# Routing pieces at the end of the first attention: exponentials traced one step later, divisions two steps later, some pieces in other steps

## The chip, the cores and the metric

The kernel runs on one core of a Trainium2 chip. The metric is the device time of one execution in microseconds. The core has five engines with a queue each: TensorE (PE, whose weight loads appear as PEld), VectorE (DVE), ScalarE (ACT), GpSimd (POOL) and SyncE (SP, which issues the DMAs). An instruction starts when it is at the head of its engine's queue and its semaphore waits are met, so an instruction that waits holds all that stand behind it on that engine.

## The reference

Two layers act on x, of shape (8, 256, 256) in float32, each an attention and a feed-forward part added to x. The change lies where the first attention (layer 0, 16 heads of 16) ends and the first mixture of experts begins to be routed. What matters of the reference:

```python
def _L0_ffn_ref(x, norm_gamma, slot_norm_gamma, slot_embeds, w1, b1, w2, b2):
    xn = rmsnorm(x, norm_gamma)
    sn = rmsnorm(slot_embeds, slot_norm_gamma)
    logits = jnp.einsum('bnd,esd->bnes', xn, sn)
    dispatch = jax.nn.softmax(logits, axis=1)
    b, n, e, s = logits.shape
    combine = jax.nn.softmax(logits.reshape(b, n, e * s), axis=-1)
    slots = jnp.einsum('bnd,bnes->besd', xn, dispatch)
    h = jnp.einsum('besd,edh->besh', slots, w1) + b1[None, :, None, :]
    h = jax.nn.gelu(h, approximate=False)
    eo = jnp.einsum('besh,ehd->besd', h, w2) + b2[None, :, None, :]
    out = jnp.einsum('bmd,bnm->bnd', eo.reshape(b, e * s, -1), combine)
    return out

x = x + _L0_xattn_ref(_layernorm(x, axis=-1), ctx_768, ...)
x = x + _L0_ffn_ref(_layernorm(x, axis=-1), ...)
x = x + _L1_xattn_ref(_layernorm(x, axis=-1), ctx_768, ...)
x = x + _L1_ffn_ref(_layernorm(x, axis=-1), ...)
```

There are 8 experts with 128 slots each, so the logits of a batch are 256 tokens x 1024 slots. The routing of one batch is two softmaxes over them: one along the slots for each token (combine), one along the tokens for each slot (dispatch), and from the second the contents of the slots.

## The kernel before

All of x stays in SBUF (x_sb). The program runs layer 0's attention for 8 batches, then the mixture of experts in 4 groups of 2 batches, then layer 1's attention and its feed-forward part.

**The loop of the first attention.** The outer loop `for h in range(8 * B + 12)` (from L868) makes 76 steps. A step h traces: `scores` (L525), which holds TensorE's scores of step h by query (for the row maxima, NM on DVE) and by key (for step h-6, whose exponentials ex on ACT are L573); `turn_back`; the second halves of pieces begun in the step before (`for f in halves`); every fourth step `pair_maxima` (nm on TensorE, added to QT on DVE); the pieces that `whole` lists for step h, entered with `at(h, f)`; and every fourth step `values` (o on TensorE, zt and rz on DVE, zs on POOL). From step 64 on there are only scores by key, from step 70 on none.

**What sets the order.** Instructions made through `matmul`, `transpose` and, inside the loop, `vec` (DVE) and `gps` (POOL) are kept in program order on their engine, and so are the score exponentials. Other ACT instructions (the copies and, before, the routing's exponentials) and operations made after the loop, such as the scaling xh_moe of later batches (through `normed`, L233), are placed by a scheduler, which can bring them forward among the loop's. All through `vec` and `gps` are recorded under L103, so tiles tell them apart. Readers of one PSUM tile on different engines take turns: each waits for the one before it.

**PSUM.** Scores use two buffers ("big"). All else that TensorE writes in the loop, but o, shares three 128x512 buffers (`ps_mm`); a group waits until the buffer that it takes has been read.

**The routing of batches 0 and 1 (`routing0`, L729)** is spread over steps 43 to 75 as pieces. A plan is a string: a letter for the piece, the step, and arguments after the point. For each batch:

- N (`scale`): xh_moe, the normalized tokens, two operations on POOL.
- P (`prepare`): four transposes pt_xm, two scaled copies xnT on DVE.
- T (`by_token` t, m): logits ln of token half t and slot half m; maximum nmn on DVE; copy of the logits on ACT into se (L760); with m = 1 the minimum of both negated maxima, two exponentials of 512 columns with their sums (L766), the sum zn and its inverse rzn on DVE.
- U (`turn_token` t): eight transposes ptn, two copies to CT, one on ACT (L784) and one on DVE.
- S (`by_slot` q, h): four transposes ls of the copied logits of both token halves, maxima nms on DVE, two exponentials of 256 columns (L807), the inverse of their sums (zs) on DVE, and the division by it on POOL.
- D (`turn_slot` q): eight transposes pts, two copies on ACT (L830) into the tile wq.
- F (`fill` q, c): two matmuls pf, then four scaled writes into the slots, alternately on ACT (L848) and DVE.

The exponentials go in turn into three parts of tiles that the attention no longer needs: two halves of krows and wk. `slot_scaled` and `slot_piece` make the scaled transposed slot embeddings snT, `moe_mean` the means and variances of later groups' tokens (bst, mvp), and `moe_scale_newton` their scales: three instructions on DVE and then sixteen small ones on POOL (nt, ny, scl). The weights of the first expert are loaded in step 50. After the loop the experts begin (ph, L1060; ht on ACT, L1068, which needs another activation table).

**Where the steps lie in the profiled execution.** Step 47's scores start at 161.12 us, step 50's at 173.54, step 54's at 189.44, step 55's at 194.22, step 60's at 212.84, step 63's at 226.92, step 66's at 235.43, step 69's at 247.74, and the first ph at 271.71.

Of the kernel before, what the change touches and what calls it, by code (L numbers as in the profile page):

```python
# [8 lines left out]
F32 = mybir.dt.float32  # L9
# [6 lines left out]
P = 128  # L16
# [47 lines left out]
def kernel(ctx: ExitStack, tc: tile.TileContext, a: dict, out: bass.AP):  # L64
# [219 lines left out]
    with ExitStack() as l0:  # L284
# [444 lines left out]
        def routing0(b):  # L729
# [14 lines left out]
            def by_token(t, m):  # L744
# [16 lines left out]
                if m == 1:  # L761
                    vec.tensor_tensor(nm[:, 2:3], nm[:, 0:1], nm[:, 1:2], ALU.min)
                    en = st[f"en{t}"] = next_em()
                    z = stat.tile([P, 4], F32, tag="zm", bufs=4, name=f"zn_{b}_{t}")
                    for i in range(2):
                        nc.scalar.activation(  # L766
                            en[:, i * 512 : (i + 1) * 512],
                            lgs[t][i],
                            AF.Exp,
                            bias=nm[:, 2:3],  # L770
                            accum_out=z[:, i : i + 1],
                        )
                    vec.tensor_tensor(z[:, 2:3], z[:, 0:1], z[:, 1:2], ALU.add)
                    vec.reciprocal(rzn0[:, 2 * b + t : 2 * b + t + 1], z[:, 2:3])
# [14 lines left out]
            def by_slot(q, h):  # L789

                if h == 0:
                    st[f"es{q}"] = next_em().rearrange("p (i n) -> p i n", i=4)
                    st["nms"] = stat.tile([P, 4], F32, tag="nm", bufs=4, name=f"nms_{b}_{q}")
                    st["zs"] = stat.tile([P, 4], F32, tag="zm", bufs=4, name=f"zs_{b}_{q}")
                es, nm, z = st[f"es{q}"], st["nms"], st["zs"]
# [9 lines left out]
                for i in range(2):  # L805
                    k = 2 * h + i
                    nc.scalar.activation(  # L807
                        es[:, k, :],
                        pl[:, i, :],
                        AF.Exp,  # L810
                        bias=nm[:, k : k + 1],
                        accum_out=z[:, k : k + 1],
                    )
                vec.reciprocal(z[:, ks], z[:, ks])
                gps.tensor_tensor(
                    es[:, ks, :],
                    es[:, ks, :],
# [844 lines left out]
```

## Time and profile before

| | us |
|---|---|
| median of 3 runs (lowest, highest) | 1348.21 (1345.59, 1351.38) |
| time of the profiled execution | 1348.56 |
| its span, first to last instruction | 1346.8 |
| busy PE / PEld | 1316.7 / 955.1 |
| busy DVE / ACT / POOL | 562.4 / 582.1 / 245.1 |
| mean granted clock | 0.997 |

A line of the profile names the engine, the kernel's line, the operation, the tiles written and read, and the sizes. What stands in brackets at the end of a row of the timeline is the idle time of that engine before the row, and whose work ended it. A row of the waits gives the waiting engine, tile and line, what it waited for, the total in us, how often, and the longest. A row of the windows gives start and end in us, the length, the busy time and instruction count of each engine, the mean granted TensorE clock (1.00 is full), the DMAs' busy share, and GB/s. Rows of PE count passes, of which one matmul in float32 has two or more, so "x4" can be two instructions.

### The profile page before, as it was taken

The page shows a single profiled execution, that of the slowest core. Times are in us where ns is not written, and L with a number is a line of the kernel's source. Part 1 is how long each engine was busy: PE and PEld are TensorE (multiplying, and loading weights), DVE is VectorE, ACT ScalarE, POOL GpSimd, SP SyncE. Part 2 cuts the span into 40 slices and gives each one's busy share as a digit, 9 for nine tenths or more (in the row PEclk, how much of TensorE's full clock was granted, in tenths as well). Part 3 has the DMA queues.
Part 4 walks back from the last instruction along what each step waited for, and adds up shares of the span by engine and source line. Part 5 has one row for each costly group of instructions (what it writes and reads, how often), then busy time and mean ns, then how long its engine had stood idle before and what let it go on. Part 6 is the DMA issues. An engine that isn't in the chain of part 4 may idle for free.

```text
span 1346.8 us, 19104 instructions
## 1 busy us (share of the span) xinstructions
PE 1316.7 (98%) x7520; PEld 955.1 (71%) x7520; DVE 562.4 (42%) x1118; ACT 582.1 (43%) x1406; POOL 245.1 (18%) x285
## 2 busy tenths in 40 slices
PE   8999989799999999999999999999999999999998
PEld 5666655477778877878768788876666676677777
DVE  6677766423330233321333110024545444544675
ACT  2644455544432263522625222213546445444653
POOL 3232401301010000100001000011333323333423
PEclk9999998999999999999999999999999999999999
DMA  7100000033325232432323425350000000000001
GB/s 220 60 1 2 1 1 1 1 106 125 107 93 178 88 105 96 133 129 71 129 71 133 133 67 187 113 153 1 1 1 1 1 0 1 1 1 1 1 8 55
DMA packets 59129, 86.85 MB, mean 64 GB/s; under 512 B 3360, under 2 KB 49056, under 8 KB 59040
## 3 DMA queue, kind: packets, MB, share of 16 engines
q1 hardware_dynamic: 58464, 85.11, 19.4%
q8 instruction: 59, 0.97, 0.3%
q10 hardware_dynamic: 576, 0.52, 0.1%
q14 instruction: 30, 0.25, 0.1%
HBM read 83.53 MB, written 2.10 MB: 64 GB/s over the span
## 4 chain that ended last, share of the span: by engine, by line
PE 91%; ACT 4%; DVE 3%; POOL 1%; issue 1%; DMA 1%; ACTq 0%; DVEq 0%; POOLq 0%
PE ph L1060 17%; PE pe L1076 16%; PE sc L74 9%; PE q L74 6%; PE o L74 6%; PE po L74 5%; PE k L74 5%; PE pe L77 4%; PE v L74 4%; PE pc L1102 4%; PE ln L924 3%; PE pf L1006 3%; PE pk L74 1%; PE pr L74 1%; PE pf L74 1%; PE pv L74 1%
## 5 line engine op out<-in xcount | busy, mean ns | idle before, releaser
L1068 ACT ACTIVATE ht<-ph,b 128x256 f32<-128x256 f32 x256 | 119.3, 474 | 372.1 <-PE ph L1060 371.7
L1060 PE MATMUL ph<-slots,w 128*128 128x256 f32 x1024 | 266.6, 384 | 1.9 <-ACT ht L1068 1.4
L1076 PE MATMUL pe<-w,ht 128*128 128x256 f32 x1024 | 263.1, 381 | 0.0
L1060 PEld LDWEIGHTS ph<-slots,w 128*128 128x128 f32 x1024 | 182.3, 189 | 55.0 <-ACT ht L1068 22.3
L1076 PEld LDWEIGHTS pe<-w,ht 128*128 128x128 f32 x1024 | 192.1, 190 | 29.9 <-DVE slots L1085 4.2
L1335 POOL TENSOR_TENSOR ex<-ex,rz 128x1024 f32<-128x1024 f32 x64 | 119.8, 1893 | 230.0 <-DVE rz L1333 222.5
L1322 ACT ACTIVATE ex<-sc,nm 128x256 f32<-128x256 f32 x256 | 117.4, 484 | 53.0 <-DVE nm L1317 53.0
L74 PE MATMUL sc<-KT,QT 17*128 17x256 f32 (+1 forms) x1024 | 103.3, 382 | 0.9 <-ACT QT L517 0.9
L984 POOL TENSOR_TENSOR es<-es,zs 128x1024 f32<-128x1024 f32 x12 | 22.7, 1893 | 444.8 <-DVE zs L983 444.8
L573 ACT ACTIVATE ex<-sc 128x512 f32<-128x512 f32 x128 | 75.2, 597 | 63.7 <-PE sc L74 56.8
L103 DVE TENSOR_REDUCE NM<-sc 128x2 f32<-128x512 f32 x128 | 86.5, 688 | 34.3 <-PE sc L74 30.3
L1085 DVE TENSOR_TENSOR slots<-pe,b 128x512 f32<-128x512 f32 x32 | 22.1, 692 | 185.1 <-PE pe L1076 185.1
L74 PE MATMUL q<-xT,wq 128*128 128x256 f32 x384 | 94.9, 391 | 0.9 <-DVE xT L1232 0.9
L74 PEld LDWEIGHTS sc<-KT,QT 17*128 17x128 f32 (+1 forms) x1024 | 75.8, 187 | 20.7 <-issue 11.6
L74 PEld LDWEIGHTS q<-xT,wq 128*128 128x128 f32 x384 | 69.2, 189 | 28.1 <-issue 15.2
L1317 DVE TENSOR_REDUCE nm<-sc 128x4 f32<-128x1024 f32 x64 | 75.4, 1219 | 7.7 <-PE sc L74 4.7
L74 PE MATMUL po<-wo,ot 128*128 128x256 f32 x320 | 72.5, 382 | 0.0
L77 PE MATMUL pe<-ident,ex 128*128 128x128 f32 x512 | 70.1, 278 | 0.8 <-DVE et L1351 0.7
L74 PEld LDWEIGHTS po<-wo,ot 128*128 128x128 f32 x320 | 60.1, 190 | 10.9 <-issue 3.2
L77 PEld LDWEIGHTS pe<-ident,ex 128*128 128x128 f32 x512 | 56.4, 140 | 15.3 <-issue 7.6
L1351 ACT COPY et<-pe 128x512 f32<-128x512 f32 x64 | 37.5, 598 | 63.9 <-PE pe L77 63.4
L74 PE MATMUL o<-et,V 128*64 128x256 f32 x512 | 62.8, 385 | 0.8 <-ACT ot L1370 0.8
(224 smaller groups left out, 1668.9 us busy)
## 6 DMA issues: line engine op xcount, KB each, us to landing
w<-in_w_dram SPq DMA_DIRECT2D x64, 1024.0 KB, 5.6
b<-in_b_dram SPq DMA_DIRECT2D x32, 128.0 KB, 6.8
x_sb<-in_x_dram SPq DMA_DIRECT2D x3, 512.0 KB, 6.0
ctx0T<-in_ctxT_dram SPq DMA_DIRECT2D x4, 256.0 KB, 8.2
ctx1T<-in_ctxT_dram SPq DMA_DIRECT2D x8, 128.0 KB, 7.9
se<-in_slots_dram SPq DMA_DIRECT2D x1, 1024.0 KB, 10.2
wq<-in_wq_dram SPq DMA_DIRECT2D x1, 1024.0 KB, 5.0
wo<-in_wo_dram SPq DMA_DIRECT2D x1, 1024.0 KB, 12.5
```

Of the source, the lines that this page charges most:

```text
L74: tc.keep_in_program_order(nc.tensor.matmul(out, lhsT=lhsT, rhs=rhs, start=start, stop=stop))
L77: tc.keep_in_program_order(nc.tensor.transpose(out, in_, ident))
L103: ins = op(*args, **kwargs)
L573: nc.scalar.activation(ex[:, 2 - 2 * i : 4 - 2 * i, :], sc[1 - i][:, :, 1, :], AF.Exp)
L924: nc.tensor.matmul(pl[:, m * 512 : (m + 1) * 512], lhsT=st["xnT"][:, c, t * P : (t + 1) * P], rhs=snT[:, c, m * 512 : (m + 1) * 512], star ...
L1060: nc.tensor.matmul(ph, lhsT=c_["w1"][:, c, hc * P : (hc + 1) * P], rhs=slots[e][:, c * 256 : (c + 1) * 256], start=(c == 0), stop=(c == 1),)
L1068: nc.scalar.activation(ht, ph, AF.Gelu, bias=b1[:, e, hc : hc + 1])
L1076: nc.tensor.matmul(c_["pe"][:, b, :], lhsT=c_["ht"][hc][:, b * SL : (b + 1) * SL], rhs=c_["w2"][:, hc, :], start=(hc == 0), stop=(hc == HI ...
L1102: nc.tensor.matmul(pc[:, :D], lhsT=CT[:, bl, e, t * P : (t + 1) * P], rhs=eos[e][:, bl, :], start=(e == 0), stop=(e == E - 1),)
L1317: nc.vector.tensor_reduce(nm, sc, AX.X, ALU.max, negate=True)
L1322: nc.scalar.activation(ex[:, i, qb, :], sc[:, i, qb, :], AF.Exp, bias=nm[:, i, qb : qb + 1], accum_out=z[:, i, qb : qb + 1],)
L1335: nc.gpsimd.tensor_tensor(ex, ex, rz.rearrange("p h q -> p (h q)").unsqueeze(2).to_broadcast([P, 4, S]), ALU.mult,)
```

## The change

`by_token` and `by_slot` no longer issue their exponentials where they are traced. They return a function that the loop runs in the next step, behind that step's scores and score exponentials; it issues the routing's exponentials, now kept in program order on ACT, and returns a second function (the sum and inverse, or the inverse and the division), which the loop runs one step later still. The exponentials' PSUM tile of `by_slot` is read one step later, accordingly. In `fill`, the four writes of a call go to one engine: DVE for batch 1 and for batch 0 where c equals q, else ACT. In `turn_slot`, the second copy of batch 1 goes to DVE. The steps of pieces change: the slot pieces of experts 6 and 7 (sn and pt_sn) come from steps 47 and 49 to 43 and 45, `moe_scale_newton(1)` from 68 to 63 and `moe_scale_newton(2)` from 71 to 75, two pieces of `moe_mean` by two steps, and the plans as the diff shows.

```diff
         for e2 in range(4):
-            at(23 + 8 * e2, lambda e2=e2: slot_scaled(e2))
-            at(25 + 8 * e2, lambda e2=e2: slot_piece(e2))
-        for g, when in enumerate(((29, 31, 37, 39), (45, 47, 53, 61), (61, 64, 65, 66))):
+            at((23, 31, 39, 43)[e2], lambda e2=e2: slot_scaled(e2))
+            at((25, 33, 41, 45)[e2], lambda e2=e2: slot_piece(e2))
+        for g, when in enumerate(((29, 31, 37, 39), (47, 49, 53, 61), (61, 64, 65, 66))):
...
-        at(68, lambda: moe_scale_newton(1))
-        at(71, lambda: moe_scale_newton(2))
+        at(63, lambda: moe_scale_newton(1))
+        at(75, lambda: moe_scale_newton(2))
...
                 vec.tensor_reduce(nm[:, m : m + 1], pl, AX.X, ALU.max, negate=True)
                 nc.scalar.copy(lgs[t][m], pl)
-                if m == 1:
-                    vec.tensor_tensor(nm[:, 2:3], nm[:, 0:1], nm[:, 1:2], ALU.min)
+                if m == 0:
+                    return None
+                vec.tensor_tensor(nm[:, 2:3], nm[:, 0:1], nm[:, 1:2], ALU.min)
+
+
+                def exponentials():
                     en = st[f"en{t}"] = next_em()
                     z = stat.tile([P, 4], F32, tag="zm", bufs=4, name=f"zn_{b}_{t}")
                     for i in range(2):
-                        nc.scalar.activation(
...
-                    vec.tensor_tensor(z[:, 2:3], z[:, 0:1], z[:, 1:2], ALU.add)
-                    vec.reciprocal(rzn0[:, 2 * b + t : 2 * b + t + 1], z[:, 2:3])
+                        tc.keep_in_program_order(
+                            nc.scalar.activation(
...
+                    def inverse():
+                        vec.tensor_tensor(z[:, 2:3], z[:, 0:1], z[:, 1:2], ALU.add)
+                        vec.reciprocal(rzn0[:, 2 * b + t : 2 * b + t + 1], z[:, 2:3])
+
+                    return inverse
+
+                return exponentials
...
             def by_slot(q, h):
...
                 vec.tensor_reduce(nm[:, ks], pl, AX.X, ALU.max, negate=True)
...
+                def exponentials():
+                    if h == 0:
+                        st[f"es{q}"] = next_em().rearrange("p (i n) -> p i n", i=4)
+                        st["zs"] = stat.tile([P, 4], F32, tag="zm", bufs=4, name=f"zs_{b}_{q}")
+                    es, z = st[f"es{q}"], st["zs"]
...
+                    def divide():
+                        vec.reciprocal(z[:, ks], z[:, ks])
+                        gps.tensor_tensor(
...
+                    return divide
+
+                return exponentials
...
-                    nc.scalar.copy(dt[:, t, :], pt)
+                    (vec.tensor_copy if b and t else nc.scalar.copy)(dt[:, t, :], pt)
...
-                    if i % 2:
+                    if b or c == q:
                         vec.tensor_scalar(slots, got, gam[:, c : c + 1], None, ALU.mult)
...
-                "N43 P47 T48.00 T49.10 S50.00 S51.01 T52.01 T53.11 U54.0 D55.0 U55.1 F56.00 F57.01 "
-                "S58.10 S59.11 D60.1 F61.10 F63.11",
-                "N59 P62 T64.00 T65.10 S66.00 S67.01 T67.01 T68.11 D69.0 U69.0 S70.10 S71.11 U71.1 "
-                "F72.00 F73.01 D74.1 F74.10 F75.11",
+                "N43 P47 T48.00 T49.10 S50.00 S51.01 T52.01 T53.11 D54.0 U55.0 U55.1 F56.00 F57.01 "
+                "S58.10 S59.11 D62.1 F63.10 F65.11",
+                "N55 P60 T61.00 T64.10 S65.00 S66.01 T67.01 T68.11 D69.0 U69.0 U70.1 S70.10 S70.11 "
+                "F71.00 F72.01 D73.1 F73.10 F74.11",
...
-            for f in halves:
-                f()
+            later = [g for g in [f() for f in halves] if g]
...
-            halves = [g for g in [f() for f in whole.get(h, ())] if g]
+            halves = later + [g for g in [f() for f in whole.get(h, ())] if g]
```

More of the change, by code (lines that the diff above doesn't have):

```diff
@@ L765, in by_token @@
                     for i in range(2):
[L766 to L771, printed above, removed]
-                        )
-                    vec.tensor_tensor(z[:, 2:3], z[:, 0:1], z[:, 1:2], ALU.add)
-                    vec.reciprocal(rzn0[:, 2 * b + t : 2 * b + t + 1], z[:, 2:3])
+                        tc.keep_in_program_order(
+                            nc.scalar.activation(
+                                en[:, i * 512 : (i + 1) * 512],
+                                lgs[t][i],
+                                AF.Exp,
+                                bias=nm[:, 2:3],
+                                accum_out=z[:, i : i + 1],
+                            )
+                        )
+                    def inverse():
[3 more added lines that the diff above has]
+                return exponentials
             def turn_token(t):
@@ L791, in by_slot @@
                 if h == 0:
-                    st[f"es{q}"] = next_em().rearrange("p (i n) -> p i n", i=4)
                     st["nms"] = stat.tile([P, 4], F32, tag="nm", bufs=4, name=f"nms_{b}_{q}")
-                    st["zs"] = stat.tile([P, 4], F32, tag="zm", bufs=4, name=f"zs_{b}_{q}")
-                es, nm, z = st[f"es{q}"], st["nms"], st["zs"]
+                nm = st["nms"]
                 pl = ps_mm(f"ls_{b}_{q}_{h}").rearrange("p (i n) -> p i n", i=2)
@@ L804, in by_slot @@
                 vec.tensor_reduce(nm[:, ks], pl, AX.X, ALU.max, negate=True)
[L805 to L817, printed above, removed]
-                    z[:, ks].unsqueeze(2).to_broadcast([P, 2, S]),
-                    ALU.mult,
-                )
+                def exponentials():
[3 more added lines that the diff above has]
+                    es, z = st[f"es{q}"], st["zs"]
+                    for i in range(2):
+                        k = 2 * h + i
+                        tc.keep_in_program_order(
+                            nc.scalar.activation(
+                                es[:, k, :],
+                                pl[:, i, :],
+                                AF.Exp,
+                                bias=nm[:, k : k + 1],
+                                accum_out=z[:, k : k + 1],
+                            )
+                        )
+                    def divide():
+                        vec.reciprocal(z[:, ks], z[:, ks])
+                        gps.tensor_tensor(
+                            es[:, ks, :],
+                            es[:, ks, :],
+                            z[:, ks].unsqueeze(2).to_broadcast([P, 2, S]),
+                            ALU.mult,
+                        )
+                    return divide
+                return exponentials
             def turn_slot(q):
```

## The prediction

> **What bounds the kernel now.** I read the page first. TensorE is the bound over the whole span:
>
> ```profile
> span 1346.8 us, 19104 instructions
> PE 1316.7 (98%) x7520; PEld 955.1 (71%) x7520; DVE 562.4 (42%) x1118; ACT 582.1 (43%) x1406; POOL 245.1 (18%) x285
> ```
>
> The profiled execution took 1348.56 us, that is 1.76 around its span and 0.35 above the median of the runs (1348.21). All sums below are made against 1348.56. Adding or removing TensorE work is not part of this change, so only TensorE's idle time and its clock can move. The busy time by stretch shows where these are: TensorE is nearly full until about 165 us and again from 275.
>
> ```profile
> 155.00:165.00 10.00, 10.00 (x104) 6.49 (x100) 8.01 (x16) 5.13 (x8) 5.53 (x8) 1.00 0.01 2
> 185.00:195.00 10.00, 7.50 (x92) 4.29 (x84) 6.03 (x17) 6.64 (x15) 0.00 (x0) 1.00 0.01 2
> 215.00:225.00 10.00, 8.62 (x46) 4.48 (x46) 5.01 (x13) 4.40 (x9) 3.45 (x3) 0.66 0.01 2
> 255.00:265.00 10.00, 5.96 (x30) 2.91 (x22) 4.82 (x15) 3.51 (x12) 5.65 (x19) 1.00 0.00 0
> ```
>
> (The columns are PE, PEld, DVE, ACT, POOL, then the granted clock.) That is steps 47 to 75, which the change edits. The waits of TensorE between 155 and 275 us:
>
> ```profile
> PE sc L74 <- ACT ex L573: 3.6, 3, 1.7
> PE ptn L77 <- ACT wq L830: 2.4, 2, 1.9
> PE pf L74 <- ACT wk L807: 2.2, 1, 2.2
> PE pts L77 <- POOL wk L103: 1.6, 1, 1.6
> PE pts L77 <- POOL krows L103: 1.6, 1, 1.6
> PE ph L1060 <- ACT ht L1068: 1.1, 1, 1.1
> PE ln L74 <- DVE snT L103: 1.1, 1, 1.1
> ```
>
> With three below 0.6 they make 14.9 us. Three rows of the timelines show the rest of what I need: a queue head that waits (DVE), and the clock after a wait (PE).
>
> ```profile
> 187.80 0.16 DVE L103 TENSOR_TENSOR zn<-zn 128x1 f32<-128x1 f32 x1 [1.87 <-ACT wk L766]
> 252.74 1.38 DVE L103 TENSOR_SCALAR xh_moe<-x_sb,mvp_moe,scl 128x256 f32<-128x256 f32 x4 [3.81 <-POOL scl L103]
> 219.62 3.78 PE L74 MATMUL pf<-wq,xh_moe 128*128 128x512 f32 x4
> ```
>
> The same four pf passes take 1.88 at 199.51. Between 217 and 223 us the clock is 0.50, after 1.59 us of wait. That stretch costs 1.9 (pf), 1.0 (the sixteen score passes, 2.08 for 1.08) and 0.5 (six pts), 3.4 in all. At 247.74 eight score passes take 1.19 for 0.71, so 0.5 more. Lost now: 14.9 + 3.4 + 0.5 = 18.8.
>
> **What each part takes away.** The slot transposes pt_sn go from step 49 to 45 (0.5 us of TensorE in either place). The wait for snT, 1.06, goes. POOL scales them ahead of its Newton steps: 1.83 more there, hidden, since xh_moe was ready at 158.4 and read at 164.0.
>
> In steps 52 to 55 DVE's queue stood behind the sum zn. The chain of waits goes ex routing (1.53 on ACT), zn, the two maxima NM (1.19), one score exponential, TensorE: waits of 1.75 and 0.75. As the changed kernel is built, zn comes two steps later and the score exponentials come first. I walked each queue with the rows' durations (score exponential 0.50, routing pair 1.03 or 1.53, NM 0.60, copies 0.60, division 1.04, slots 0.27 when four follow each other). On the clock of that walk, which starts at step 47, TensorE is ready for step 54's scores at 186.2 and the last exponential of the step before at 185.7. For step 55 it is 190.2 against 188.9. So 2.5 goes; what is late next is the copy of ptn behind the score exponentials in step 55: 0.4 (0.5 now).
>
> The divisions of slots 4 to 7 end one step earlier relative to their transposes: step 60's wait of 1.59 goes, and the 3.4 of slow clock with it. The cover is thin: on the walk the second division ends near 214.9 and pts start at 215.0, so each 0.1 of lateness costs 0.1. Beside it, in step 61, two short groups (nm, pt_xm) stand ahead of the scores; where that happens now (90.94, 116.19) the scores wait 0.39 for ex. I take 0.4.
>
> Evictions: eight slots writes and two copies go from ACT to DVE, some 8 x 0.35 + 2 x 0.6 = 4.0 us on DVE and 4.1 off ACT, in stretches where DVE is busy 3 to 6 of 10. One effect is on the path: the last slots write on ACT now stands behind the table load, and ph waits 1.10 for its buffer. With these on DVE that goes. The remaining waits, 236.90 to 266.44 (8.1, and the 0.5 at 247.74), give way to the next list. One of them is the 1.63 of pts in step 74: the division of wk stood on POOL behind the sixteen operations of moe_scale_newton(2) (259.76 to 264.24). That goes to step 75, behind the last division; its reader, xh_moe_4, then holds DVE's queue until about 265, and xnT_2, the next that TensorE needs, is due near 271, so it is hidden; without that cover it costs up to the chain's 4.6. The product xh_moe of batch 1 goes to step 55 (2.43 on POOL, read in step 60, some 16 us later, hidden), the maxima pieces moe_mean (0.55 each on DVE) stay inside DVE's idle time. No DMA changes place: the expert's load stays in step 50, and SP's queue is the same.
>
> **What it adds.** First, moe_scale_newton(1) goes from step 68 to 63. As built, the first write of xh_moe_2 stands on DVE right behind the Newton start, ahead of QT0_7, nmn and the copies that follow. From ny's end to xh_moe the row above and its POOL chain (248.14 to 252.74) give 4.6 us. There ny ends 221.4, xh_moe_2 starts 226.0, QT0_7 227.0, the maximum nmn of ln_1_1_0 ends 228.5, ACT's copy se 229.1. TensorE has been ready for ls (which reads that copy) since 226.2. So 3.0 us of wait, and 0.25 at the next scores, whose exponentials queue behind the copy. If the cover were complete this were nothing; if POOL were late with zs it would be longer by as much. Today the same block stands at 248.9 to 252.7 and is partly covered.
>
> Second, steps 69 and 70 take four ptn groups in a row. ACT has, between them and the last ln, copy, exponentials, routing pair, copy, exponentials, routing pair, copy: 0.5 + 1.0 + 1.5 + 0.5 + 1.0 + 1.5 + 0.55 = 6.6 us, against 5.35 of TensorE from ln_1_0_1's end (0.75 of start-up on ACT's side): waits of 0.2 and 2.05. Third, in step 73 the divisions follow zt, ot and four slots writes on DVE (recips at 252.0), 1.04 each on POOL: pts waits 0.95 and 0.8, pf 0.15. Sum of the new waits: 0.4 + 0.4 + 3.25 + 2.25 + 1.9 = 8.2.
>
> 18.8 - 8.2 = 10.6. Each stall that goes also saves a refill of about 0.1 (13 now, 9 then): 11.0. Added up step by step, the walk gives 12.2; that is the upper end. The lower end, if every margin below 0.5 were missed by 0.5 (five places), is 8.5. At an unchanged clock: 1348.6 - 11.0 = 1337.6.
>
> **The clock.** The row at 216.38 shows that a wait of 1.59, amid transposes and score passes, halved the clock for 6.8 us; 1.75 behind ln (189.44) and 2.24 behind pf (261.44) did not. The new 3.0 wait, followed by ls, scores, ls until o starts at 231.1, is nearer to the first: I take one such stretch, 3.4. So 1341.0. [...]
>
> **The rivals.** (a) No slow stretch, 1337.6: for it speak the four longer waits without one (1.63 to 2.24); against it, that the new wait is longer than all of them.
>
> (b) Two slow stretches: steps 69 and 70 hold nothing but transposes and waits from 240.4 to 246.7. A second one costs 2.8 (3.4 less what the waits of step 73 take up): 1343.8. Against it: 248.9 to 253.3 in the trace is of the same kind, 1.89 wait included, and kept its clock; for it: the new one is 2 us longer. [...]
>
> (c) Slower than before: the clock, halved in step 65, does not recover while steps 66 to 75 stay sparse. TensorE works 26 us there; doubled, less 4.4 of waits that vanish in it, 22 us: 1359. It passes the kernel before from 22 us at half clock on (0.5 us per us). Against it: the stretch at 217 ended after 6.8 us with scores and pf alone.
>
> (d) The change does not do what it says: the score exponentials are late for another reason than the routing's place on ACT, and the waits of 1.75, 0.75 and 0.5 stay: 1341.0 + 3.0 = 1344.0. Against it is the zn row.
>
> **How the numbers follow.** Main case 0.45, (a) 0.12, (b) 0.34, (c) 0.05, (d) 0.04. About 0.5% (6.7 us) is what a measurement of this kernel can tell from no change, so faster means below 1341.5. The main case, 1341.0 with some 1.5 either way, is below it 6 times in 10: 0.28; with (a) 0.12 and 0.03 of (b), faster 0.43. Slower is (c), 0.05. Same is the rest, 0.52. The range runs from (a) less 1.2, the walk's upper end, to (b) with the 2.5 of missed margins: 1336.4 to 1346.3.
>
> **What would show it.** Right: no PE wait on snT; none on ex in steps 53 to 55; no pts wait near 215; a PE wait of about 3 on se (L760) near 226 to 229, behind a DVE wait of 4 to 4.6 on scl; clock 0.5 for about 7 us after it; a ptn wait near 2 on ACT's wq copy near 243; pts waits on POOL wk below 1; no wait of ph on ht; first ph near 264 instead of 271.7. Wrong: waits on ex left in steps 53 to 55, a covered Newton chain, or a clock row unlike the one forecast.

## The result, and the profile after

The changed kernel takes 1339.17 us (median of 6 runs, 1338.05 to 1339.90), the kernel before beside it 1348.60 (6 runs, 1345.50 to 1351.38). The ratio is 0.9933, with a 95% interval of 0.9919 to 0.9947: faster by 0.5 to 0.8%. Forecast was 1341.0. The profiled execution took 1339.66, 8.90 less than the profiled one of before. One execution of the experiments below, the profiled one of the first, ran at a mean granted clock of 0.834, 7 or 8 tenths in every slice of its page (1522.73 us), and is in no ratio.

The first lines of the page, and the waits of TensorE between 155 and 275 us (waiting engine, tile and line, what it waited for; total us, times, longest):

```profile
span 1337.9 us, 19105 instructions
...
PE 1315.6 (98%) x7520; PEld 954.9 (71%) x7520; DVE 565.3 (42%) x1128; ACT 576.8 (43%) x1396; POOL 245.7 (18%) x285
```

```profile
PE ls L77 <- ACT se L760: 1.6, 1, 1.6
PE pts L77 <- POOL wk L103: 1.6, 2, 1.0
PE ptn L77 <- ACT wq L855: 1.5, 1, 1.5
PE ls L77 <- DVE QT L103: 0.6, 1, 0.6
PE ptn L77 <- ACT CT L796: 0.4, 1, 0.4
PE sc L74 <- ACT ex L573: 0.4, 1, 0.4
PE pf L74 <- ACT wq L855: 0.3, 1, 0.3
PE ph L1084 <- ACT ht L1092: 0.2, 1, 0.2
```

They make 6.6 us where 14.9 stood. The waits on snT and on krows are gone, those on ex shrank from 3.6 to 0.4. The busy time by stretch shows the same (start and end, then PE, PEld, DVE, ACT, POOL, granted clock, DMA share, GB/s):

```profile
185.00:195.00 10.00, 9.57 (x111) 6.34 (x110) 7.98 (x20) 8.20 (x19) 4.10 (x4) 1.00 0.01 2
215.00:225.00 10.00, 10.00 (x86) 5.18 (x87) 4.55 (x12) 5.86 (x13) 3.26 (x14) 1.00 0.00 0
225.00:235.00 10.00, 7.78 (x48) 3.64 (x50) 6.18 (x18) 3.57 (x9) 0.64 (x3) 0.75 0.01 2
...
255.00:265.00 10.00, 8.16 (x32) 5.28 (x32) 5.25 (x18) 0.86 (x2) 2.93 (x7) 1.00 0.05 5
```

Between 185 and 195, TensorE went from 7.50 to 9.57 of 10. The slow clock of 215 to 225 (0.66 before) is gone, and a new one stands at 225 to 235 (0.75). The timelines of DVE and of TensorE show where that came from:

```profile
221.11 0.17 DVE L103 TENSOR_SCALAR ny_moe<-nt_moe 128x8 int32<-128x8 int32 x1
225.90 0.41 DVE L103 TENSOR_SCALAR xh_moe<-x_sb,mvp_moe,scl 128x256 f32<-128x256 f32 x1 [4.62 <-POOL scl L103]
226.22 0.68 DVE L103 TENSOR_TENSOR QT<-nm,QT 128x512 f32<-128x512 f32 x1
```

```profile
226.96 0.33 PE L77 MATMUL ls<-ident,se 128*128 128x128 f32 x1 [0.61 <-DVE QT L103]
228.89 0.55 PE L77 MATMUL ls<-ident,se 128*128 128x128 f32 x3 [1.60 <-ACT se L760]
229.39 1.71 PE L74 MATMUL sc<-QT,KT 18*128 18x256 f32 x8
231.04 1.12 PE L77 MATMUL ls<-ident,se 128*128 128x128 f32 x4
232.08 3.64 PE L74 MATMUL o<-ex,V 128*32 128x256 f32 x32
```

DVE's queue head, the first write of xh_moe_2, waits 4.62 us for POOL. QT, nmn and through it ACT's copy se are late behind it, TensorE waits 0.61 and 1.60, and right after that its passes take about twice as long (o 3.64; with the clock at 1.00, at 249.56, 1.93). The trace's record of the granted clock has one stretch at half in this part, 6.83 us long, from 229.9 on. From the sc row of 229.39 to the po that follows the next sc (236.81) 7.42 us pass; the same passes take 3.73 in the kernel without this wait (first experiment), so 3.7 are lost.

Of these 3.7, 0.5 are not the clock's. The weight loads of the sc passes wait twice 0.19 for exponentials ex, which stand on ACT behind the late copy se. The rows of the waits do not show this as a wait of TensorE's passes, but the same passes are as late at full clock, in the kernel with the evictions of before (below), where the half clock starts at 231.25:

```profile
229.53 1.19 PE L74 MATMUL sc<-QT,KT 18*128 18x256 f32 x8
```

They take 0.71 where nothing is late. So the clock costs 3.2; half speed over 6.83 us can cost no more than 3.4.

So of the 18.8 us lost before, 6.6 of waits, 0.5 at these scores and 3.2 of clock are left: 8.5 gained. With the prediction's estimate of 0.4 for refills behind waits that are no more this makes 8.9, which is the difference of the two profiles; the 0.4 was not measured by itself. The gain is there at the first ph, which begins at 263.55 instead of 271.71, and in the wait of ph behind it, 0.24 instead of 1.10.

### The profile page after: what moved, and what is told of

Same layout as the page of the kernel before. It is cut to its first block, busy times and chain, and to the rows that moved or that the text cites. A ratio compares the mean times of both kernels' runs of the same rounds, so it can differ in the third digit from the quotient of the medians.

```text
span 1337.9 us, 19105 instructions
## 1 busy us (share of the span) xinstructions
PE 1315.6 (98%) x7520; PEld 954.9 (71%) x7520; DVE 565.3 (42%) x1128; ACT 576.8 (43%) x1396; POOL 245.7 (18%) x285
## 4 chain that ended last, share of the span: by engine, by line
PE 92%; ACT 4%; DVE 2%; issue 1%; POOL 0%; DMA 0%; SPq 0%; ACTq 0%; DVEq 0%; POOLq 0%
PE ph L1084 17%; PE pe L1100 16%; PE sc L74 9%; PE o L74 7%; PE q L74 6%; PE po L74 5%; PE k L74 5%; PE pe L77 4%; PE v L74 4%; PE pc L1126 4%; PE ln L948 3%; PE pf L1030 3%; PE pk L74 1%; PE pr L74 1%; PE pv L74 1%; ACT ex L573 1%
## 5 line engine op out<-in xcount | busy, mean ns | idle before, releaser
L1359 POOL TENSOR_TENSOR ex<-ex,rz 128x1024 f32<-128x1024 f32 x64 | 119.9, 1895 | 229.9 <-DVE rz L1357 222.4
L77 PE MATMUL pe<-ident,ex 128*128 128x128 f32 x512 | 70.2, 278 | 0.8 <-DVE et L1375 0.7
L77 PEld LDWEIGHTS pe<-ident,ex 128*128 128x128 f32 x512 | 56.5, 140 | 15.3 <-issue 7.6
## 6 DMA issues: line engine op xcount, KB each, us to landing
se<-in_slots_dram SPq DMA_DIRECT2D x1, 1024.0 KB, 10.9
```

Source lines behind the costliest of these rows:

```text
L77: tc.keep_in_program_order(nc.tensor.transpose(out, in_, ident))
L1359: nc.gpsimd.tensor_tensor(ex, ex, rz.rearrange("p h q -> p (h q)").unsqueeze(2).to_broadcast([P, 4, S]), ALU.mult,)
```

## The experiments

Times are medians; ratios are to the kernel before, run beside each on the same chip, with 95% intervals. Edits are against the changed kernel where nothing else is said.

### The Newton block out of step 63

```diff
-        at(63, lambda: moe_scale_newton(1))
-        at(75, lambda: moe_scale_newton(2))
...
                 at(8 * b + 19, lambda b=b, qb=qb: project(b, qb, tos[b]))
+        at(75, lambda: moe_scale_newton(1))
+        at(75, lambda: moe_scale_newton(2))
```

> The changed kernel with moe_scale_newton(1) traced in step 75, behind the last projection, instead of in step 63. My theory: in the changed kernel this block holds DVE's queue for 4.62 us (the product xh_moe at 225.90 waits for POOL's scl), so QT, nmn and the copy se come late and TensorE waits 0.61 + 1.60 + 0.39 us near 227 to 229, and this wait is what halves the granted clock in the 6.8 us behind it (3.4 us). Both go: 1339.7 - 2.6 - 3.4 = 1333.7 us, no TensorE wait over 0.5 on DVE QT or ACT se between 215 and 232, clock above 0.95 from 220 to 240. The block at the end is hidden: xh_moe_2 is wanted some 10 us after the first ph. Rival 1: the slow clock belongs to the thin mix of transposes and score passes in steps 61 to 66, not to the wait: then only the wait goes, 1337.0 us, and a row with a clock near 0.6 stays between 215 and 240. Rival 2: the sixteen POOL operations, 4.6 us, only move: a wait of 2 to 5 us appears in front of pt_xm or ph near 265 to 275, 1336 to 1339 us.

1335.55 us, the median of five executions with the one of 1522.73 among them; the other four took 1333.75 to 1335.56, ratio 0.9904 (0.9886 to 0.9922). It was run again to read its waits.

> The same kernel as before, moe_scale_newton(1) in step 75, to read its waits: its profile was taken in an execution whose clock stood near 0.8 from end to end, and shows nothing of them. Its other executions took 1333.75 to 1335.56 us. My theory: the wait at ls is gone, no slow stretch near 225 to 240, and what is left above 1333.7 in most executions is one window of half clock (3.4 us, 1.7 us of time) near step 70, where TensorE waits for the copy wq. Rival 1: the slow stretch is still at 225 to 240 though the wait is gone, half as long. Rival 2: a wait of 1 to 2 us in front of pt_xm or ph near 262 to 275.

1335.85 us, ratio 0.9912 (0.9890 to 0.9934), executions from 1333.33 to 1336.04. TensorE has no wait left between 215 and 240; ls follows pf at once:

```profile
225.24 1.98 PE L74 MATMUL pf<-wq,xh_moe 128*128 128x512 f32 x4
227.06 0.60 PE L77 MATMUL ls<-ident,se 128*128 128x128 f32 x4
```

The clock is 1.00 there, so both rivals on that place fall: the slow stretch goes with the wait, and no wait appears in front of pt_xm or ph but the 0.24 that was there. The one stretch at half clock that this execution has in this part is the one that I named for what is left, of 3.41 us, behind the wait of 1.46 for wq in step 70. The windows' rows of this kernel around it, cut at the edges of that stretch and in steps of its length (such a length of 3.41 us is called a window below):

```profile
239.22:242.63 3.41, 1.82 (x13) 1.31 (x13) 1.71 (x4) 3.38 (x9) 0.00 (x0) 1.00 0.00 0
242.63:246.04 3.41, 3.41 (x22) 2.81 (x24) 1.94 (x3) 0.94 (x2) 0.00 (x0) 0.50 0.00 0
```

The changed kernel has the same wait of 1.46 at 246.2 to 247.6 and kept its clock there. Cut in steps of 3.41 us from the edges of its own slow stretch, the wait is split between two windows:

```profile
243.56:246.97 3.41, 2.50 (x20) 1.70 (x16) 2.11 (x6) 3.41 (x9) 0.00 (x0) 1.00 0.00 0
246.97:250.39 3.42, 2.75 (x32) 2.26 (x36) 1.94 (x5) 1.70 (x5) 0.00 (x0) 1.00 0.00 0
```

TensorE busy for 1.82 of 3.41 in one window was followed by a slow one; 2.50 and 2.75 were not. The share does not decide it alone: in the kernel with the plan alone (below) a window with 2.51 of 3.41, from 234.36 on, was followed by a slow one.

### The same block back in step 68

```diff
-        at(63, lambda: moe_scale_newton(1))
+        at(68, lambda: moe_scale_newton(1))
```

> The changed kernel with moe_scale_newton(1) back in step 68, where it stood before the change; moe_scale_newton(2) stays in step 75. My theory: the wait at ls near 227 (2.6 us) and the slow stretch behind it (3.4) go, but the block now stands on DVE ahead of the maximum nmn of ln_1_1_1. Worked out on the changed kernel's times less 6.0: POOL's division of wk ends at 236.7, its sixteen operations at 241.2, nmn runs at 242 instead of 237, and the chain on ACT behind it (se, two exponentials, the routing pair, the copy wq) ends 5 us later, so that the wait of 1.46 at ptn becomes about 6: 1339.7 - 6.0 + 5.0 = 1338.7 us if the clock holds, 1342 if the longer wait brings a slow stretch of its own. Rival: the place of the block is not what makes the wait at ls; then that wait stays at about 2.6 near 227 and the time is 1339.7 or more by what step 68 adds (about 1344).

1342.12 us, ratio 0.9956 (0.9941 to 0.9971): 3 us slower than the changed kernel, as my theory had it with a slow stretch. The wait at ls is gone, and the block holds DVE as long one place later (timelines of DVE and of TensorE):

```profile
241.47 0.74 DVE L103 TENSOR_SCALAR xh_moe<-x_sb,mvp_moe,scl 128x256 f32<-128x256 f32 x2 [4.59 <-POOL scl L103]
```

```profile
243.49 1.97 PE L77 MATMUL ptn<-ident,krows 128*128 128x128 f32 x8 [4.78 <-ACT se L760]
246.34 1.97 PE L77 MATMUL ptn<-ident,krows 128*128 128x128 f32 x8 [0.89 <-ACT wq L855]
```

The half clock begins in the longer wait, at 241.88, and lasts 10.24 us, three windows. The block holds DVE for 4.6 us in both steps; the place decides who needs DVE then. So the move from 68 to 63 was worth some 3 us with the rest of the change around it, and 63 is not the best place.

### Warming TensorE in the wait

Three matmuls of 512, 512 and 256 columns between the last pf ahead of ls (which is traced in step 65, not in 64 as the text below says) and that ls, and in another kernel eighteen 128x128 transposes:

```diff
+            def keep_warm():
+                pw = ps_o(f"warm_{b}")
+                for n in (512, 512, 256):
+                    matmul(pw[:, :n], lhsT=ident, rhs=snT[:, 0, :n], start=True, stop=True)
...
-                "N55 P60 T61.00 T64.10 S65.00 S66.01 T67.01 T68.11 D69.0 U69.0 U70.1 S70.10 S70.11 "
+                "N55 P60 T61.00 T64.10 W65 S65.00 S66.01 T67.01 T68.11 D69.0 U69.0 U70.1 S70.10 S70.11 "
```

> The changed kernel with three more matmuls, 512 + 512 + 256 columns (about 2.2 us), put on TensorE between the product pf of step 64 and ls of step 65, into a PSUM tile that nobody reads: they fill the time in which TensorE waits for QT and se. Nothing else changes. My theory: the half clock behind that wait comes from TensorE standing still there, in windows of 3.4 us; with the matmuls it does not come, the waits stay, and all executions are near 1339.7 - 3.4 = 1336.3 us (the changed kernel's own executions of 1338.05, with one window, would give the same 1336.35). Rival: the clock goes down because the work around it is thin (score passes, transposes), or for another engine's sake; then a slow stretch stays and the time is 1338.0 to 1339.9 as without them.

> As the run with three more matmuls, but eighteen transposes of 128x128 (about 2.1 us) in the same place. If transposes count as work for the clock as matmuls do, 1336.3 us and no slow stretch. If they do not (this is what I hold likelier, 0.6, since 1.59 us of wait among transposes and score passes halved the clock in the kernel before and 2.24 us behind four pf passes did not), the slow stretch stays: 1338.0 to 1339.9 us, as in the changed kernel.

1338.11 us with matmuls (1336.39 to 1338.62), 1337.12 with transposes (1336.81 to 1338.85); both 0.993 of the kernel before, as the changed kernel is, so that the ratios do not tell the three apart. In both profiles the clock at this place is 1.00. Here are the filled wait (timeline of TensorE) and the clock's window behind it (windows), with matmuls first:

```profile
226.79 2.31 PE L74 MATMUL warm<-snT,ident 128*128 128x512 f32 x6
228.94 0.27 PE L77 MATMUL ls<-ident,se 128*128 128x128 f32 x1
229.50 0.55 PE L77 MATMUL ls<-ident,se 128*128 128x128 f32 x3 [0.28 <-ACT se L760]
```

```profile
228.45:231.86 3.41, 3.13 (x23) 1.81 (x25) 3.38 (x11) 2.14 (x5) 0.00 (x0) 1.00 0.02 5
```

and with transposes:

```profile
226.87 2.13 PE L77 MATMUL warm<-ident,snT 128*128 128x128 f32 x18
```

```profile
228.98:232.40 3.42, 2.95 (x29) 1.75 (x31) 3.35 (x12) 2.56 (x6) 0.00 (x0) 1.00 0.02 5
```

The same DVE and ACT lateness with a busy TensorE gives no slow clock here. The profiles of all runs together bear this out. Four kernels have the wait of 0.6 and 1.6 at ls (the changed one, and those with the plan alone, with moe_scale_newton(2) back in step 71 and with the old evictions, below); in all four half clock follows within 2.6 us of its end, for 6.83 us in the first and 3.41 in the other three. Six have no such wait or have it filled (the block in step 75 or 68, the two warmed ones, the two at the end); in none does half clock begin between 215 and 241 us. So TensorE standing still is what the half clock needs there, and the thin mix of score passes and transposes behind it alone does not bring it. That answers the rival of the run with matmuls.

My leaning on transposes (0.6 that they would not count) was wrong. By estimate the changed kernel without half clock would take 1336.4 (1339.66 less 3.2), and none of its six executions came under 1338.05; with the transposes four of six lie at 1336.81 to 1337.28. The window that the transposes fill holds some 1.4 us of pf as well, but the last kernel below has a clearer one. From 238.92 to 242.33 TensorE is busy for 3.22 of 3.41 us there, 2.43 of them transposes (L77) and the rest o, and the clock stays at 1.00; in the changed kernel half clock followed on a window with 1.34 (226.50 to 229.91). The place of the windows in the last kernel is an estimate, counted back in whole windows from the half clock at the program's end; in the changed kernel that one begins 1105.92 us after the stretch at 229.91, which is 324 times 3.4133.

The "all executions near 1336.3" was wrong too. The profiled executions of both have one window of half clock elsewhere, from 245.5 and from 256.2, behind the waits of steps 70 and 73, where the changed kernel's profile had none.

### The deferral and the plan, each alone

The steps, pieces and evictions of the changed kernel, with exponentials and divisions issued where they are traced, and the routing's exponentials no longer held in program order on ACT:

```diff
-                        tc.keep_in_program_order(
+                        (
                             nc.scalar.activation(
...
-                return exponentials
+                exponentials()()
```

> The changed kernel's steps, pieces and evictions, but routing exponentials, score exponentials of the routing and divisions issued where they are traced, as before the change, and not held in program order. My theory: what the later exponentials do is to take the sum zn out of DVE's queue in steps 52 to 55. So TensorE's waits on ex (1.75 and 0.75 us in the kernel before, near 189 and 194) come back, 2.5 us, and the wait of 0.43 at ptn goes: 1339.7 + 2.1 = 1341.8 us; the pts wait near 215 stays away, since the transposes stand two steps later than before and the division now comes earlier still. Rival: the deferral carries most of the gain (divisions included), then 1345 us or more.

1343.66 us, ratio 0.9970 (0.9956 to 0.9983), 1.9 above the forecast and 1.3 below its rival. The zn block is back as foretold (DVE, then TensorE):

```profile
186.34 0.16 DVE L103 TENSOR_TENSOR zn<-zn 128x1 f32<-128x1 f32 x1 [1.87 <-ACT wk L771]
```

```profile
187.97 0.71 PE L74 MATMUL sc<-QT,KT 18*128 18x256 f32 x8 [1.75 <-ACT ex L573]
```

Only this one of the two waits came back in steps 54 and 55; two more on ex, 1.37 in step 61 and 0.74 in step 69, and one of 1.11 at pts took the other's place. All waits sum to 8.7, 2.1 more than in the changed kernel, which is the sum that I had foretold, put together otherwise. It has one window of half clock more (three), which is what the forecast left out. Its executions took 1340.87 to 1346.28. How much of the loss belongs to the later place and how much to the program order was not tried apart.

The kernel before with the deferral alone (the same functions, called one and two steps later):

```diff
-                "S58.10 S59.11 D60.1 F61.10 F63.11",
+                "S58.10 S59.11 D61.1 F62.10 F63.11",
...
-            for f in halves:
-                f()
+            later = [g for g in [f() for f in halves] if g]
...
-            halves = [g for g in [f() for f in whole.get(h, ())] if g]
+            halves = later + [g for g in [f() for f in whole.get(h, ())] if g]
```

> The kernel before with the deferral alone: routing exponentials a step later and behind the score exponentials, divisions two steps later; steps, pieces and evictions as before, except that the slot transposes of batch 0's second half go from step 60 to 61 and their product from 61 to 62 (without it the transposes would be ahead of their own division). My theory: the waits on ex near 189 and 194 (2.5 us) go, but every division now ends later against transposes that did not move as far: the pts wait near 215 (1.59) becomes 2 to 3.5, with its slow stretch, and pts in steps 69 to 74 wait longer by 1 to 3 in all. 1348.6 - 2.5 + 1 + 2 = 1349, within 1346 to 1351 us: alone it brings nothing. Rival: the deferral is the gain by itself, 1341 to 1343 us.

1356.15 us, ratio 1.0058 (1.0043 to 1.0073): slower than before by 7.6, and 5 past my range. The waits on ex are 0.8 in all, as expected. What I had missed stands in step 69 (DVE, then TensorE):

```profile
250.45 0.73 DVE L103 TENSOR_SCALAR xh_moe<-x_sb,mvp_moe,scl 128x256 f32<-128x256 f32 x2 [4.59 <-POOL scl L103]
...
252.09 0.16 DVE L103 RECIPROCAL zs<-zs 128x2 f32<-128x2 f32 x1
```

```profile
253.51 1.54 PE L77 MATMUL pts<-ident,wk 128*128 128x128 f32 x6 [6.43 <-POOL wk L103]
```

The inverse zs, traced two steps later, falls in behind the Newton block of step 68 on DVE, and its division waits for it. Yet the waits of TensorE up to the first experts sum to 16.1, only 1.2 more than before. Half clock lasts 23.9 us in three stretches, against 6.83 in one, so that, by difference, some 5 of the 6.4 between the two profiles are the clock's. The waits on POOL wk still make 9.3 of the 16.1, and two of the three stretches begin in them or right behind. I took the blocks out:

```diff
-        at(68, lambda: moe_scale_newton(1))
-        at(71, lambda: moe_scale_newton(2))
...
+        at(75, lambda: moe_scale_newton(1))
+        at(75, lambda: moe_scale_newton(2))
```

> The kernel with the deferral alone (1356.15 us), and both Newton blocks moved to step 75 behind the last projection. My theory: the deferral alone was slower because the divisions of wk, traced two steps later, came to stand on POOL behind the sixteen operations of the Newton blocks (245.9 to 250.4 and 262.8 to 267.3 in its trace, pts waiting 6.43 and 2.35 + 0.56). With the blocks gone these become at most 0.5 and about 1.5, and of the two slow stretches behind them (6.8 us each) at least one goes: 1356.2 - 6 - 1.5 - 3.4 = 1345.3, within 1343 to 1347 us. The waits on krows (2.3) and its slow stretch of 10.2 us near 214 to 224 stay. Rival: the divisions are late by being traced two steps later, whatever stands ahead of them on POOL; then 1352 us or more.

1350.38 us, ratio 1.0020 (1.0008 to 1.0032). The wait of 6.43 is gone and 5.8 us with it, so the rival (1352 or more) falls; but I had expected 10.9. Here the last slots writes still alternate and come behind the last projection, so in step 75 they queue on DVE behind the block that I had put there (DVE, then TensorE):

```profile
274.23 0.41 DVE L103 TENSOR_SCALAR xh_moe<-x_sb,mvp_moe,scl 128x256 f32<-128x256 f32 x1 [0.41 <-POOL scl L103]
...
274.63 0.35 DVE L103 TENSOR_SCALAR slots<-pf,gam 128x128 f32<-128x128 f32 x1
```

```profile
276.35 4.30 PE L1084 MATMUL ph<-slots,w 128*128 128x256 f32 x12 [2.33 <-DVE slots L103]
```

That is 2.3 of wait and a window of half clock, and a wait of 2.0 at ptn has come up as well. Alone, then, the plan with its evictions gives 4.9 us, the deferral loses 7.6, and both together gain 9.4: the deferral needs the plan. Taking the blocks out of the old plan is not enough (1.0020 of the kernel before).

### moe_scale_newton(2) back in step 71

```diff
-        at(75, lambda: moe_scale_newton(2))
+        at(71, lambda: moe_scale_newton(2))
```

> The changed kernel with moe_scale_newton(2) alone back in step 71. My theory, as in the prediction (the cover of step 75 costs up to the chain's 4.6 us when it is taken away): its sixteen POOL operations stand ahead of the divisions of wk, which end 2.8 to 3.8 us later, so the first pts wait in step 73 is 4 to 5 us instead of 0.99, with one or two windows of half clock behind it: 1339.2 + 3.3 + 1.7 = 1344.2, within 1342 to 1346 us. Rival: POOL has time for both (it is busy 2 of 10 us there) and the time stays at 1339 to 1340 us.

1344.50 us, ratio 0.9974 (0.9963 to 0.9986), as foretold. The wait at pts in step 73 is 4.77 instead of 0.99, and 6.83 us of half clock follow (behind the wait at ls there is one window of it, where the changed kernel's profile has two):

```profile
258.12 0.67 PE L77 MATMUL pts<-ident,wk 128*128 128x128 f32 x2 [4.77 <-POOL wk L103]
```

This one line of the change is worth 5.3 us, more than half of the gain. Step 75 hides the block: the changed kernel's list of TensorE's waits between 262 and 320 us has the 0.24 at ph alone.

### The evictions of before

```diff
-                    (vec.tensor_copy if b and t else nc.scalar.copy)(dt[:, t, :], pt)
+                    nc.scalar.copy(dt[:, t, :], pt)
...
-                    if b or c == q:
+                    if i % 2:
```

> The changed kernel with the evictions as before it: the copies of pts on ACT alone, slots writes alternating between DVE and ACT. My theory: the last slots write goes back behind ACT's table load, so that ph waits 1.1 instead of 0.24 (+0.9), and ACT, whose queue makes ptn wait 1.46 in step 70, gets one more copy of 0.6 ahead of it and two slots writes in steps 62 to 64 (+0.6): 1339.2 + 1.5 = 1340.7 us. Rival: DVE was made late by the evictions that it took over (its queue stands for 4.6 us in step 65 and makes TensorE wait there); with fewer operations on it the waits at ls and ptn shrink, and the time is at or under 1338 us.

1340.19 us, ratio 0.9957 (0.9942 to 0.9972), about 1 us slower, which the intervals do not tell apart (and its profile has one window of half clock less). The part on ACT's queue came: ptn waits 2.20 instead of 1.46. The part on ph did not; its wait stays 0.24 (TensorE, then ACT):

```profile
246.24 1.63 PE L77 MATMUL ptn<-ident,krows 128*128 128x128 f32 x12 [2.20 <-ACT wq L855]
...
265.89 1.13 PE L1084 MATMUL ph<-slots,w 128*128 128x256 f32 x4 [0.24 <-ACT ht L1092]
```

```profile
262.15 0.37 ACT L873 ACTIVATE slots<-pf,gam 128x128 f32<-128x128 f32 x1 [0.42 <-DVE slots L103]
264.07 1.28 ACT L1092 ACT_TABLE_LOAD   x1 [1.55 <-PE ph L1084]
```

The last slots write is on ACT again and still 1.9 us ahead of the table load: the new plan has both products of slots 4 to 7 in front of the projection po (F73.10 F74.11; before, F75.11 came behind it). So the engine of the writes did not take the 1.10 away. The order of the products is what I see that did; with the old order and the old evictions, in the kernel before and in the two of the deferral alone, ph waits 1.10. The order was not put back by itself.

### Toward a faster one

The Newton blocks late, the second ptn pair behind the slot scores, and the first product a step later, so that DVE's inverses come ahead of its slots writes:

```diff
-                "N55 P60 T61.00 T64.10 S65.00 S66.01 T67.01 T68.11 D69.0 U69.0 U70.1 S70.10 S70.11 "
-                "F71.00 F72.01 D73.1 F73.10 F74.11",
+                "N55 P60 T61.00 T64.10 S65.00 S66.01 T67.01 T68.11 D69.0 U69.0 S70.10 S70.11 U71.1 "
+                "F72.00 F72.01 D73.1 F73.10 F74.11",
```

> The changed kernel with moe_scale_newton(1) and (2) in step 75 behind the last projection, the second pair of ptn groups (turn_token of the second half) in step 71 behind the slot scores and o instead of in step 70, and the first product pf of the second half in step 72 instead of 71, so that DVE's reciprocals for wk stand ahead of its slots writes. My theory, on the trace of the kernel with the Newton block moved alone: the wait of 1.46 at ptn in step 70 comes from three exponential pairs in a row on ACT and goes when slot scores and o (2.9 us) are put between; POOL's divisions of wk end 2.9 us earlier against pts, so their waits of 1.0 and 0.6 shrink to about 0.3. 1335.8 - 1.5 - 1.3 = 1333.0 us, and 1331.3 where the window of half clock near step 70 stays out too. Rival: the reordering only hands the wait on (the copies of CT or of wq late for pf, the division still last): 1335 us or more.

1334.23 us, ratio 0.9893 (0.9876 to 0.9910). The pts waits of 1.6 became one of 0.6, but the 1.46 was handed on, as the rival said, though to another group than it named (and the time stayed under its 1335): the group behind ptn is now ls, and it wants the same buffer of the three that all these groups share.

```profile
241.96 1.62 PE L77 MATMUL ls<-ident,se 128*128 128x128 f32 x8 [1.46 <-ACT wq L855]
```

So the copy that frees the buffer went to DVE, which idles there (0.75 us of it ahead of 240.54):

```diff
-                    (vec.tensor_copy if b and t else nc.scalar.copy)(dt[:, t, :], pt)
+                    (vec.tensor_copy if b and (t or q == 0) else nc.scalar.copy)(dt[:, t, :], pt)
```

> The kernel with the Newton blocks late, the ptn groups apart and the divisions ahead of the slots writes (1334.23 us), and one copy more on DVE: wq<-pts of slots 4 to 7 in step 69, which there stands on ACT behind the routing pair of step 69 (it ends at 241.9) and makes ls wait 1.46 for its buffer. On DVE it runs at 239.0 to 239.6, in a stretch in which DVE is idle. My theory: the wait at ls becomes 0.1 to 0.3: 1334.2 - 1.2 = 1333.0 us, and 1331.2 where no window of half clock comes. Rival: the copy CT on ACT behind the same routing pair is late next (ptn_1_1 or o waits as long), 1334 us and more.

1331.04 us (1330.75 to 1333.62), ratio 0.9879 (0.9857 to 0.9902): 8 us faster than the changed kernel, 17.5 faster than the one before. The largest waits that TensorE has left between 155 and 275 us:

```profile
PE ptn L77 <- ACT CT L796: 0.4, 1, 0.4
PE pts L77 <- POOL wk L103: 0.4, 1, 0.4
PE sc L74 <- ACT ex L573: 0.4, 1, 0.4
```

The six that are left make under 2 us, and its profiled execution (1331.27) has no stretch at half clock there at all.

## Why the prediction was right or wrong

The direction, the range and the main case's picture (one new wait, one slow stretch behind it) held. 1341.0 was 1.8 too high, a little outside the 1.5 that I had given the main case. By the prediction's own line (below 1341.5) the kernel is faster, which it gave 0.43; no change it gave 0.52. Step by step:

| term | forecast | measured |
|---|---|---|
| waits on snT, on ex in steps 54 and 55, on krows with its slow clock | gone | gone |
| next late in step 55: copy of ptn | 0.4 | 0.43 |
| scores of step 61, behind nm and pt_xm | 0.4 | 0.39 |
| DVE's wait for scl; start of xh_moe_2 | 4.6; 226.0 | 4.62; 225.90 |
| step 65: waits at ls, lateness of the scores behind it | 3.0 + 0.25 | 0.61 + 1.60, 0.5 at the scores |
| slow clock behind it | one stretch, 3.4 | one, 6.83 us long, 3.2 |
| ptn in steps 69 and 70 | 0.2 + 2.05 | 1.46 |
| step 73: pts, pts, pf | 0.95 + 0.8 + 0.15 | 0.99 + 0.56 + 0.29 |
| ph on ht | gone | 0.24 |
| first ph | 264 | 263.55 |

**The two mis-sized terms.** New waits were to sum to 8.2; with the 0.5 at the scores of step 65 they sum to 7.1. Of the difference 0.5 lies in step 65 and 0.8 at ptn; the rest is less than 0.3 either way. In step 65 I had the copy se end 0.3 later than it did, TensorE ready 0.15 earlier, and its whole first ls group waiting; in truth its first pass needs only the buffer that QT frees, and ran (0.33) inside the wait. That makes the wait 0.8 shorter, and the scores behind it were late by 0.25 more than I had. (The prediction had seen this lateness of scores at 247.74 in the kernel before, 1.19 for 0.71, and counted 0.5.) At ptn I gave ACT 6.6 us of work against 5.35 of TensorE; from the copy se (241.28) to the end of the copy wq (247.6) it was 6.3, and TensorE from the end of ln_1_0_1 (240.45) to its wait (246.18) 5.7. With 1.1 less of waits and 0.2 less of clock, the forecast's own sum gives 1339.7, the time of the profile. That sum has 0.1 in it for each refill behind a stall, which no run shows by itself; what the rows of the changed kernel show is that passes that wait for nothing can overlap those ahead of them (by 0.17 where the scores of 214.35 follow those of 213.81, by 0.07 where pts follows at 214.89). Three of the six executions took 1338.05 to 1338.68, at a mean granted clock of 0.998 to 0.999 instead of 0.997; one window of half clock less (half of 3.41 us, 0.0013 of the span) would make that difference, which is not shown, since only one execution was profiled.

**The step with the wrong cause.** "With these on DVE that goes": the wait of ph went, but not for that reason. With the old evictions it stays away; the order of the last products is the likely cause.

**The cover of step 75.** The prediction said that without it moe_scale_newton(2) would cost up to 4.6 of wait. Put back it costs 3.6 more of wait (4.77 + 0.33 for 0.99 + 0.56) and a slow stretch, 5.3 in time; and the kernel in which both blocks stand in step 75 shows the cover to hold even for sixteen more POOL operations. It is a cover only where the last slots writes are ahead of the block; in the kernel with the deferral alone and the blocks late they are not, and ph waited 2.33.

**The clock.** Main case (one stretch at step 65) right, and that it comes from the wait, not from the mix of work, is shown by the ten profiles with and without it. The prediction took its length, 6.8 us, from the row at 216.38. That the length came out the same is luck: three other kernels with the same wait have one window behind it, 3.41 us, and not two. Rival (a), no slow stretch, fell in the profile: 2.2 us of wait were enough. Even the 1.46 in step 70 was followed by 3.41 us of half clock in three profiles (the block in step 75, the matmuls put in, and the first of the two kernels at the end). Rival (b), a second stretch in steps 69 and 70, did not come in the profile of the changed kernel, but it came in the same steps in these three, for the same wait of 1.46. So (b) names a thing that can happen for this wait. That it would be for the transposes, which the expectation of the eighteen holds likelier, is not what these and the window of the last kernel show: as this kernel makes them (products with the identity, in the rows of L77), the clock stayed at 1.00 behind 2.13 us of them and behind a window with 2.43. Rival (c), no recovery, is excluded by full clock from 236.7 on. Rival (d), the deferral not doing what it says, is excluded by the scores of steps 54 and 55, which no longer wait for ex; in the kernel without it those of step 54 wait behind zn again.

## What to carry to other kernels

A piece whose head waits for another engine's long chain (here sixteen small POOL operations behind three on DVE) held its queue for the whole chain, 4.6 us, in both steps of the loop that were tried. So place it where nobody needs that queue, and check each instruction that a deferral makes fall in behind it: the same deferral lost 7.6 us in the old plan and helped to gain 9.4 in the new one. When the wait on a shared buffer was moved, the next group in turn had it, until the copy that frees the buffer went to an idle engine. Here waits of 1.46 to 2.2 us had 3.41 or 6.83 us of half clock behind them in some profiles and none in others, so such a wait is priced at its length plus, with some chance, half of such a stretch; filling it with TensorE work, transposes too, removed the second part here (clock 1.00 behind 2.31 us of matmuls and behind 2.13 us of transposes).

## What the runs showed of the hardware

**The half clock comes in whole windows of one length.** The stretches in the traces are 3.41, 6.83 and 10.24 us long, that is 1, 2 and 3 times 3.413. Where a trace has several, they begin whole windows apart: 8 and 6 in the kernel with the plan alone (189.98, 217.29, 237.77), 11 and 5 in the one with the deferral alone (214.09, 251.64, 268.70), 324 in the changed kernel and 331 in the one before, from the stretch in this part to the half clock at the program's end (1105.92 and 1129.81 us). The same wait of 1.46 cost a window in three profiles and nothing in the changed kernel's, where it lay across the edge between two. The spread of the kernel before goes with the clock: beside the experiments, its executions with a mean granted clock of 0.999 or 1.000 took 1344.52 to 1347.14, those with 0.994 or 0.995 took 1348.57 to 1351.53. That the place of the waits against the windows' edges makes this difference is argued, not shown, since I did not control that place.

**What decides whether half clock follows stays open.** A window in which TensorE was idle for about half was followed by half clock in some cases, and in others not. In the kernel before, these two windows differ little in TensorE's share, yet the first was followed by half clock and the second was not:

```profile
213.26:216.67 3.41, 1.82 (x25) 1.25 (x18) 2.26 (x5) 2.11 (x6) 1.39 (x2) 1.00 0.00 0
...
250.80:254.21 3.41, 1.94 (x24) 1.39 (x28) 1.45 (x5) 2.39 (x5) 1.41 (x7) 1.00 0.00 0
257.63:261.04 3.41, 1.57 (x4) 0.38 (x2) 1.66 (x7) 0.67 (x3) 1.99 (x7) 1.00 0.00 0
```

Nor was the third, with only 1.57, all of it pf passes of 512 columns. The share alone does not decide; what else does was tried no further than in the two warmed kernels.

**The start of the kernel varies by 0.9 us.** The transposes pt_x begin at 7.38 us in the changed kernel's profile and at 8.26 in that of the kernel with the Newton blocks moved, whose start is the same code: the first four k passes took 2.58 instead of 1.95, and the sixteen passes ahead of them 3.68 instead of 3.31. Differences of less than 1 us between two profiles should be read at one place late in the program, against one place early.
